# A two-layer transformer step on one core: attention's side products moved between scores and sums

## The chip, the cores and the metric

The kernel runs on one core of a Trainium2 chip, in one launch. The metric is the device time of the execution in microseconds; the median of three runs is given.

## The reference, cut to what matters

Input x has shape (2, 2048, 256). Two layers follow, each of the form x + attention(norm(x)) + ffn(norm(x)). The first has a gated linear attention and a quantised linear layer. The change lies in the second, whose attention has 16 heads of 16 columns with a linear bias by distance, one half of the heads looking back and the other forward; its other half is a mixture of 8 experts, two for each token, chosen by 20 rounds of row and column normalisation (Sinkhorn):

```
# attention
scores = einsum('bhqd,bhkd->bhqk', q, k) * (1.0 / sqrt(16)) + bias
out = einsum('bhqk,bhkd->bhqd', softmax(scores), v)
out = out.transpose(0, 2, 1, 3).reshape(B, S, D) @ Wf + bf
# experts
pi = _sinkhorn(-(xf @ gate_W.T))          # 20 rounds: rows, then columns
_, top_idx = top_k(pi, 2)
y = einsum('enf,edf->end', silu(g) * u, W_down)
out = sum over k of y[top_idx[:, k], n] * pi[:, k]
```

The second layer's result is x plus both, in float32.

## The kernel before

The span has three parts. The first layer, with the projections of the second layer's queries, keys and values at its end, takes up to about 432 us. The second layer's attention takes from there to about 830 us. The experts follow to the end.

**Units.** `_units()` (L1609) cuts the attention into 150 units. A unit has four rows, one for each head of a group of four, and each row has up to 512 query columns (`WIDE`), packed from pieces of up to 256 queries against 128 keys. The loop at L1944 to L1979 takes the units in order. Nothing reorders the work: each engine has it in the order in which the loop issues it, and for VectorE (`vector`, an `InOrder` wrapper whose calls show as L121) and most of GpSimd's sends program order is pinned. Names:

- `scores` (L1817) multiplies keys and queries for the four rows into four PSUM banks (`sc`, matmuls of L1823), and issues the exponentials on ScalarE from there to `pt` (L1832). Row 0's exponential is in two parts.
- `keep_only` (L1835) takes the minimum of the diagonal blocks of `pt` and a mask on VectorE. A unit has 0 to 12 of them.
- `weighted_sums` (L1841) multiplies `pt` by the values into one of two other banks (`o_ps`, L1846).
- `add_up` (L1860) does this for the unit two back (`LATE` is 2). Where a group of four heads has ended with that unit, it transposes the sums to `o_sb` on VectorE, and with the second group of a step it appends a chore, `normalise` (L1793), and runs its first part: reciprocal `inv`, product `on` and transposition `onT`, all on VectorE.
- `do_chore` (L1881) runs the rest of the oldest chore: the output product `f_ps` (16 recorded matmuls through `by_columns`, L1544), its addition to `acc` on VectorE and, for the second half of the heads, a store of two row tiles of the output from SP (L1815). There are 32 chores.
- `background` is the router: `DirectSinkhorn` (L1547), which in each of its 20 rounds has the steps "reciprocal of the row sums `sk_rows`, product, column sums `sk_c`" and "product with a matrix of ones into `sk_ps`, reciprocal `sk_columns`, product, next row sums `sk_r`", and then `routing.steps` (with one product, `place_ps`). `decision` follows, with one product (`d_ps`), and `sends` scatters the table's rows from GpSimd. One step is taken in a unit, and none while the masks of the unit before are more than 7 (`CALM`).
- `value_bias` (L1727) has one product, `b_ps`, a quarter of the way through.

**Banks.** PSUM has eight banks here: two for sums and six in one round, tag "mm" of the pool `ps_m` (L1713). Each new tile takes the next bank of the round, and waits until the readers of the tile that had it six tiles ago are done. Four tiles go to each unit's scores; every side product (`f_ps`, `sk_ps`, `b_ps`, `place_ps`, `d_ps`) takes one too.

**Order in a unit before.** On TensorE: scores of unit n; sums of unit n-2; the output product, if a chore was there before this unit's sums; the router's product. On VectorE: masks of unit n-1; transpositions and the chain to `onT` of unit n-2, if a group ended; the addition to `acc`; the router's or the decision's step.

Of the kernel before, what the change touches and what calls it, by code (L numbers as in the profile page):

```python
# [56 lines left out]
F32 = mybir.dt.float32  # L57
# [7 lines left out]
P = 128  # L65
B, N, E = 2, 2048, 256
# [46 lines left out]
class InOrder:  # L113


    def __init__(self, tc, engine):
        self.tc, self.engine = tc, engine
# [6 lines left out]
class LayerNorm:  # L124
# [7 lines left out]
    def tile(self, name, shape):  # L132
        name = f"ln_{name}{self.name}"
        return self.pool.tile(shape, F32, tag=name, name=name)
# [1471 lines left out]
        yield  # L1606


def _units():  # L1609

    tiles = QT // P

    def pieces_of(way, group, r, qt):  # L1620


        found = [(qt * 2 + way, 0, QT, P * way), (qt * 2 + 1 - way, P * (1 - way), P, 0)]
        slope = _slopes()[PLACES[(2 * way + group) * 4 + r] % (H1 // 2)]
        reach = math.ceil((104 + LIMIT - SHIFT) / slope) + 1
        for j in range(1, tiles * (N // QT - 1 - qt if way else qt) + 1):


            width = min(QT, reach - 1 - P * (j - 1))
            if width > 0:  # L1630
                width = -(-width // 32) * 32
                kb = qt * tiles + tiles - 1 + j if way else qt * tiles - j
                found.append((kb, QT - width if way else 0, width, None))
        return found

    steps = [(b, way, qt) for b in range(B) for way in range(2) for qt in ORDERS[way]]
    parts = [(step, group, n % 2) for n, step in enumerate(steps) for group in range(2)]
    rows = []
    for r in range(4):
        row = deque()  # L1640
        for n, ((b, way, qt), group, bank) in enumerate(parts):
            row.append((n, deque(pieces_of(way, group, r, qt))))
        rows.append(row)
    units = []
    done, begun = [[None] * len(parts) for _ in range(4)], set()
    while any(rows):
        this = len(units)
        left, masks = [deque() for _ in range(4)], []
        for r, row in enumerate(rows):
            at = slots = 0  # L1650
            while row and at < WIDE:
                n, found = row[0]
                b, way, qt = parts[n][0]
                if n >= OPEN and any(d[n - OPEN] is None or d[n - OPEN] == this for d in done):
                    break
                first = (r, n) not in begun


                def fits(width):
                    return width <= WIDE - at and max(P, width) <= SLOTS - slots  # L1660

                part = min(WIDE - at, SLOTS - slots) // P * P
                if found[0][0] == qt * 2 + way:
                    m, now = 0, found[0][2] if fits(found[0][2]) else part
                else:
                    whole = [m for m, piece in enumerate(found) if fits(piece[2])]
                    wide = whole or [m for m, piece in enumerate(found) if piece[2] - part >= P]
                    if not wide:
                        break
                    m = max(wide, key=lambda m: found[m][2])  # L1670
                    now = found[m][2] if whole else part
                if not now:
                    break
                begun.add((r, n))
                found.rotate(-m)
                kb, q0, width, diagonal = found.popleft()
                if now < width:
                    rest = None if diagonal is None else diagonal - now
                    found.appendleft((kb, q0 + now, width - now, rest))
                if not found:  # L1680
                    done[r][n] = this
                    row.popleft()
                left[r].append((r, *parts[n], kb, q0, q0 + now, at, first, not found))
                if diagonal is not None:
                    m0, m1 = max(diagonal, 0), min(diagonal + P, now)
                    if m0 < m1:
                        masks.append((r, parts[n][0][1], at + m0, m1 - m0, m0 - diagonal))
                at, slots = at + now, slots + max(P, now)
        widths = [sum(piece[6] - piece[5] for piece in pieces) for pieces in left]
        taken, pieces = [0] * 4, []  # L1690
        while any(left):
            r = min((r for r in range(4) if left[r]), key=lambda r: taken[r])
            piece = left[r].popleft()
            taken[r] += max(P, piece[6] - piece[5])
            pieces.append(piece)
        ended = [part for n, part in enumerate(parts)
                 if all(d[n] is not None for d in done) and max(d[n] for d in done) == this]
        units.append((pieces, widths, masks, ended))
    return units
# [3 lines left out]
def attention(  # L1703
# [9 lines left out]
    ps_m = ctx.enter_context(tc.tile_pool(name="aps_m", bufs=6, space=PSUM))  # L1713
    ident = c.ident

    values = operands.values
    other_values = w.tile([P, TPB, 7 * VC + HR], F32, tag="va1", name="va1")
    mask, wf, pi, grown = ready.mask, ready.wf, ready.pi, ready.grown
    for g in (2, 3):
# [7 lines left out]
    def value_bias():  # L1727


        vector.tensor_copy(ready.bvb, ready.bv.unsqueeze(2).to_broadcast([P, 2, P]))  # L1730
        yield
        ps = ps_m.tile([P, E], F32, tag="mm", name="b_ps")
        for e in range(2):
            nc.tensor.matmul(
                ps, lhsT=ready.bvb[:, e, :], rhs=wf[:, e, :], start=e == 0, stop=e == 1
            )
        vector.tensor_tensor(c.half_bias, c.half_bias, ps, ALU.add)
        vector.tensor_scalar(c.half_bias, c.half_bias, 0.5, None, ALU.mult)
        yield

    def router():
        yield from DirectSinkhorn(nc, vector, p2, ps_m, la, pi, grown, c.ones_mat).steps()
        yield from routing.steps(p2, ps_m, pi)

    def decide():
        yield from routing.blocks(p2)
# [22 lines left out]
        vector.tensor_tensor(within, within, least, ALU.mult)  # L1769
        yield  # L1770
        yield
        ps = ps_m.tile([1, P + 1], F32, tag="mm", name="d_ps")
        nc.tensor.matmul(ps[:, 0:P], lhsT=high, rhs=ident, start=True, stop=True)
        nc.tensor.matmul(
            ps[:, P : P + 1], lhsT=within, rhs=c.ones_mat[:, 0:1], start=True, stop=True
# [17 lines left out]
    def normalise(b, way, qt, turned):  # L1793


        inv = p2.tile([P, 2, QT // HR], F32, tag="inv", name="inv")
        vector.reciprocal(inv, turned[:, :, :, HD])
        on = p2.tile([P, QT // HR, 2, HD], F32, tag="on", name="on")
        vector.tensor_tensor(
            on.rearrange("p j g d -> p g j d"), turned[:, :, :, 0:HD],  # L1800
            inv.unsqueeze(3).to_broadcast([P, 2, QT // HR, HD]), ALU.mult,
        )
        onT = p2.tile([P, QT], F32, tag="onT", name="onT")
        vector.transpose(onT, on.rearrange("p j g d -> p (j g d)"))
        yield
        ts = slice(b * TPB + qt * 2, b * TPB + qt * 2 + 2)
        ps = ps_m.tile([P, 2, E], F32, tag="mm", name="f_ps")
        for n in range(2):
            by_columns(
                nc.tensor.matmul, ps[:, n, :], onT[:, n * P : (n + 1) * P], wf[:, way, :],  # L1810
                start=True, stop=True,
            )
        vector.tensor_tensor(acc[:, ts, :], acc[:, ts, :], ps, ALU.add)
        if way:
            nc.sync.dma_start(out=c.out_v[:, ts, :], in_=acc[:, ts, :])  # L1815

    def scores(pieces, widths):  # L1817
# [9 lines left out]
        for r, width in enumerate(widths):  # L1827
            ends = [at + q1 - q0 for row, *_, q0, q1, at, _, _ in pieces if row == r] if not r else []
            half = min(ends, key=lambda end: abs(end - WIDE // 2), default=width)
            for part in (slice(0, half), slice(half, width)):  # L1830
                if part.start < part.stop:
                    nc.scalar.activation(pt[:, r, part], scs[r][:, part], AF.Exp)  # L1832
        return pt

    def keep_only(pt, masks):  # L1835

# [18 lines left out]
    chores, background, sends = deque(), router(), routing.sends()  # L1855
    decision = decide()
    waiting, copies = deque(), {}
    routed, unmasked = False, None

    def add_up():  # L1860
        pieces, pt, ended = waiting.popleft()
# [19 lines left out]
    def do_chore():  # L1881
        for _ in chores.popleft():
            pass
# [58 lines left out]
    experts = Experts(tc, a, out, c, rooms, range(FULLS), range(GROUPS))  # L1942
    ahead = experts.todo[0:2]
    for n, (pieces, widths, masks, ended) in enumerate(units):  # L1944
        if n in (len(units) // 4 - 4, len(units) // 4):
            next(bias)
        if n == len(units) - BEGIN:
            for left in (background, decision, sends):
                for _ in left:
# [7 lines left out]
                block.fetch_rows()  # L1957
        if len(units) - FETCH < n <= len(units) - FETCH + 4:
            ahead[0].combine(0, range(n - len(units) + FETCH - 1, n - len(units) + FETCH))
        pt = scores(pieces, widths)  # L1960
        calm = not unmasked or len(unmasked[1]) <= CALM
        if unmasked:
            keep_only(*unmasked)
        unmasked = pt, masks
        before = len(chores)
        waiting.append((pieces, pt, ended))
        if len(waiting) > LATE:
            add_up()
        if before and chores:
            do_chore()  # L1970
        if routed:
            for _ in range(1 + n % 2):
                next(sends, None)
            if calm:
                next(decision, None)
        elif calm:
            routed = next(background, True) is True
        if n == len(units) - 4:
            ahead[0].open_rows()  # L1979
    keep_only(*unmasked)  # L1980
# [828 lines left out]
```

## Time and profile before

| | |
|---|---|
| three runs | 1500.48, 1505.16, 1506.82 us (median 1505.16) |
| profiled execution | 1507.06 us, its span 1504.8 us |
| attention's window, 432 to 830 us | PE busy 389.47, PEld 287.27, DVE 275.34, ACT 313.91 us of 398 |
| granted TensorE clock | 0.983 over the span, 0.97 in the window |
| exponentials `pt` from `sc`, 128x512 | 381 of 612 ns |
| masks on `pt`, 128x128 | 512, 283 ns each when counted singly |
| output products `f_ps` | 32 times 16 matmuls |
| Sinkhorn products `sk_ps` | 20 times 8 matmuls |
| transposition, reciprocal, product, transposition (`o_sb`, `inv`, `on`, `onT`) | 446, 254, 425, 445 ns |
| addition `acc`, 128x512 | 681 ns |

Busy time is that of the records: a matmul's end is modelled, so a busy PE is not one that never waits. PEld is TensorE's weight loads, whose starts show when the engine moved from one phase to the next. "A <- B" in a view of waits means that A was idle until B ended. Idle time of an engine that is not the bound costs nothing.

### The profile page before, as it was taken

Reading aid. Unit: us, or ns where it says so; the run is one execution under the profiler, and the core shown is the slowest. Engines: PE = TensorE matmul, PEld = TensorE weight load, DVE = VectorE, ACT = ScalarE, POOL = GpSimd, SP = SyncE. Lnnn points to the kernel's source line nnn. Section 1 sums busy time; section 2 is a strip of 40 time slices with the busy share of each in tenths; the row PEclk is TensorE's granted clock in tenths of the full one; section 3 lists DMA queues with packets and bytes.
Section 4 is the critical chain, followed back from the end, with each engine's and each line's share of the span. In section 5 each row is a group of like instructions: output and inputs, shape, how many; then the busy total and the mean of one; then the engine's idle time right before and its main releaser. Section 6 shows DMA issues by size and latency. Waiting matters only on the chain.

```text
span 1504.8 us, 33474 instructions
## 1 busy us (share of the span) xinstructions
PE 1444.7 (96%) x13712; PEld 1180.6 (78%) x13712; DVE 1009.7 (67%) x2567; ACT 730.3 (49%) x1557; POOL 538.4 (36%) x449
## 2 busy tenths in 40 slices
PE   7879999999989999999999999999999999999996
PEld 4656767676757777777666899989899998989995
DVE  6788677565448888874445767667666776666663
ACT  4444554555367888888876332333232332323231
POOL 4342222121120000399961234343434544343432
PEclk9999999999989999999999999999999999999998
DMA  8001010410353120420034656575766867576531
GB/s 236 0 15 59 30 57 30 120 58 29 81 151 60 31 62 25 95 35 5 5 131 157 224 195 199 191 286 175 261 198 218 252 210 254 193 253 241 174 83 23
DMA packets 75986, 191.94 MB, mean 128 GB/s; under 512 B 19136, under 2 KB 56768, under 8 KB 63360
## 3 DMA queue, kind: packets, MB, share of 16 engines
q0 software_dynamic: 28256, 144.23, 28.8%
q1 hardware_dynamic: 46464, 44.30, 11.9%
q8 instruction: 110, 1.80, 0.5%
q10 hardware_dynamic: 1104, 1.18, 0.3%
q14 instruction: 52, 0.43, 0.1%
HBM read 157.95 MB, written 32.10 MB: 126 GB/s over the span
## 4 chain that ended last, share of the span: by engine, by line
PE 56%; DVE 2%; ACT 1%; issue 1%; POOL 0%; POOLq 0%; another core or an unknown queue 0%
PE h_ps L121 26%; PE y_ps L121 15%; PE sc L1823 6%; PE o_ps L1846 5%; PE f_ps L1544 1%; PE h_ps L2491 1%; PE x_ps L121 1%; DVE pt L121 1%; ACT pt L1832 1%; PE h_ps L2526 0%; DVE o_sb L121 0%; ACT larger L121 0%; DVE onT L121 0%; DVE on L121 0%; DVE larger L121 0%
## 5 line engine op out<-in xcount | busy, mean ns | idle before, releaser
L1832 ACT ACTIVATE pt<-sc 128x512 f32<-128x512 f32 (+5 forms) x746 | 312.4, 517 | 78.2 <-issue 39.2
L1823 PE MATMUL sc<-qk 32*128 32x256 f32 (+3 forms) x3022 | 208.1, 361 | 3.6 <-ACT pt L1832 1.6
L121 DVE TENSOR_TENSOR larger<-larger,h_ps 128x512 f32<-128x512 f32 x160 | 109.9, 687 | 144.3 <-ACT larger L121 79.0
L1823 PEld LDWEIGHTS sc<-qk 32*128 32x128 f32 x3022 | 158.9, 189 | 46.1 <-ACT pt L1832 25.3
L121 PE MATMUL y_ps<-qk,larger 128*128 128x256 f32 x704 | 173.4, 380 | 0.3 <-DVE larger L121 0.3
L1846 PE MATMUL o_ps<-pt,va 128*32 128x256 f32 (+3 forms) x3022 | 166.2, 341 | 3.2 <-DVE o_sb L121 1.9
L121 ACT COPY larger<-h_ps 128x512 f32<-128x512 f32 x128 | 74.5, 582 | 172.7 <-PE h_ps L121 168.2
L121 DVE TENSOR_TENSOR pt<-pt,keepmask 128x128 f32<-128x128 f32 x512 | 117.4, 283 | 48.0 <-ACT pt L1832 46.9
L2405 POOL DMA_INDIRECT out<-va,to x64 | 102.7, 1604 | 124.3 <-DVE larger L121 49.1
L1846 PEld LDWEIGHTS o_ps<-pt,va 128*32 128x32 f32 x3022 | 103.3, 111 | 51.0 <-issue 20.8
L2222 POOL DMA_INDIRECT table<-rows,place x64 | 68.2, 1066 | 194.1 <-DVE pt L121 181.7
L121 PEld LDWEIGHTS y_ps<-qk,larger 128*128 128x128 f32 x704 | 123.9, 191 | 12.3 <-DVE larger L121 0.7
L121 PEld LDWEIGHTS h_ps<-va,qk 128*128 128x128 f32 x1024 | 126.6, 192 | 7.6 <-ACT larger L121 2.3
L121 PE MATMUL h_ps<-va,qk 128*128 128x128 f32 x1024 | 130.6, 276 | 1.9 <-ACT larger L121 1.9
L2568 POOL DMA_INDIRECT xb<-normed,to x64 | 65.5, 1024 | 140.5 <-DVE by L2291 71.8
L121 ACT ACTIVATE larger<-larger 128x512 f32<-128x512 f32 x64 | 40.4, 632 | 117.8 <-DVE larger L121 117.8
L121 ACT ACTIVATE va<-va 128x512 f32<-128x512 f32 x64 | 40.4, 632 | 100.2 <-DVE va L121 96.3
L121 PE MATMUL y_ps<-larger 128*128 128x256 f32 x320 | 79.0, 380 | 0.0
L121 POOL TENSOR_TENSOR pause<-ones_mat,expo 128x4 f32<-128x4 f32 x64 | 68.6, 1072 | 2.0
L121 ACT COPY va<-h_ps 128x512 f32<-128x512 f32 x64 | 36.9, 577 | 56.4 <-PE h_ps L121 51.1
L121 PE MATMUL h_ps<-larger,qk 128*128 128x128 f32 x512 | 62.7, 276 | 0.0
L121 PEld LDWEIGHTS h_ps<-larger,qk 128*128 128x128 f32 x512 | 59.7, 192 | 2.1 <-issue 2.1
(318 smaller groups left out, 2798.5 us busy)
## 6 DMA issues: line engine op xcount, KB each, us to landing
qk<-qk SPq DMA_DIRECT2D x32, 256.0 KB
qk<-qk SPq DMA_DIRECT2D x64, 128.0 KB
va<-v SPq DMA_DIRECT2D x4, 1208.0 KB
v<-v SPq DMA_DIRECT2D x8, 574.0 KB
normed<-xn SPq DMA_DIRECT2D x8, 512.0 KB
out<-acc SPq DMA_DIRECT2D x16, 256.0 KB
acc<-in_x SPq DMA_DIRECT2D x7, 512.0 KB
table<-rows,place POOLq DMA_INDIRECT x64
```

Source lines behind the costliest of these rows:

```text
L121: return lambda *a, **k: self.tc.keep_in_program_order(begin(*a, **k))
L1544: multiply(out[r : r + HR], left[:, r : r + HR], *args, **how)
L1823: nc.tensor.matmul(scs[r][:, at : at + q1 - q0], lhsT=heads[rows, 1, kb * P : (kb + 1) * P], rhs=heads[rows, 0, qt * QT + q0 : qt * QT + q ...
L1832: nc.scalar.activation(pt[:, r, part], scs[r][:, part], AF.Exp)
L1846: nc.tensor.matmul(sums[bank][r * HR : (r + 1) * HR, to + q0 : to + q1], lhsT=values[b, way][:, kb, h * VC : h * VC + HR], rhs=pt[:, r, at ...
L2222: send = self.tc.keep_in_program_order(self.nc.gpsimd.indirect_dma_start(out=self.c.table, in_=self.rows[:, t, :], in_offset=None, out_off ...
L2405: send = e.nc.gpsimd.indirect_dma_start(out=e.out, in_=y[:, c, :], in_offset=None, out_offset=bass.IndirectOffsetOnAxis(ap=self.to[:, c : ...
L2491: self.e.nc.tensor.matmul(ps[rows, :], lhsT=self.xT[:, c * P + r * SB : c * P + (r + 1) * SB], rhs=self.w[:, r, at : at + ST], start=c == ...
L2568: self.nc.gpsimd.indirect_dma_start(out=to, out_offset=None, in_=self.c.normed, in_offset=bass.IndirectOffsetOnAxis(ap=at, axis=0),)
```

## The change

A small class, `Spare`, stands in for the pool where side products ask for a bank. While a unit is worked on it holds the banks of rows 2 and 3 of the scores of the unit before; a side product takes the first that is left, and where there is none it takes one of the round as before. The list is emptied at the end of each unit. The six banks of the round thus go to scores alone, and in the order of the round the spare banks are those that the next unit's rows 0 and 1 take.

The order in a unit changes too. The bias product, the router's or the decision's step and then the chore come right after the masks, all ahead of `add_up`. So on TensorE it is now: scores of unit n, router's product, output product, sums of unit n-2. On VectorE: masks of unit n-1; router's or decision's step; addition to `acc`; transpositions and chain of unit n-2.

```diff
+class Spare:
+    def __init__(self, pool):
+        self.pool, self.banks = pool, []
+
+    def tile(self, shape, dt=F32, tag=None, name=None):
+        if not self.banks:
+            return self.pool.tile(shape, dt, tag=tag, name=name)
+        bank = self.banks.pop(0)[0 : shape[0], 0 : math.prod(shape[1:])]
+        return bank if len(shape) == 2 else bank.rearrange("p (a b) -> p a b", a=shape[1])
...
-    values = operands.values
+    values, spare = operands.values, Spare(ps_m)
...
-        ps = ps_m.tile([P, E], F32, tag="mm", name="b_ps")
+        ps = spare.tile([P, E], F32, tag="mm", name="b_ps")
...
-        yield from DirectSinkhorn(nc, vector, p2, ps_m, la, pi, grown, c.ones_mat).steps()
-        yield from routing.steps(p2, ps_m, pi)
+        yield from DirectSinkhorn(nc, vector, p2, spare, la, pi, grown, c.ones_mat).steps()
+        yield from routing.steps(p2, spare, pi)
...
-        ps = ps_m.tile([1, P + 1], F32, tag="mm", name="d_ps")
+        ps = spare.tile([1, P + 1], F32, tag="mm", name="d_ps")
...
-        ps = ps_m.tile([P, 2, E], F32, tag="mm", name="f_ps")
+        ps = spare.tile([P, 2, E], F32, tag="mm", name="f_ps")
...
-        return pt
+        return pt, scs
...
     for n, (pieces, widths, masks, ended) in enumerate(units):
-        if n in (len(units) // 4 - 4, len(units) // 4):
-            next(bias)
...
-        pt = scores(pieces, widths)
+        pt, scs = scores(pieces, widths)
+        spare.banks, behind = [bank for bank in behind[2:] if bank is not None], scs
         calm = not unmasked or len(unmasked[1]) <= CALM
         if unmasked:
             keep_only(*unmasked)
         unmasked = pt, masks
-        before = len(chores)
-        waiting.append((pieces, pt, ended))
-        if len(waiting) > LATE:
-            add_up()
-        if before and chores:
-            do_chore()
+        if n in (len(units) // 4 - 4, len(units) // 4):
+            next(bias)
         if routed:
             for _ in range(1 + n % 2):
                 next(sends, None)
             if calm:
                 next(decision, None)
         elif calm:
             routed = next(background, True) is True
+        if chores:
+            do_chore()
+        waiting.append((pieces, pt, ended))
+        if len(waiting) > LATE:
+            add_up()
+        spare.banks = []
```

More of the change, by code (lines that the diff above doesn't have):

```diff
@@ L1857, in attention @@
     waiting, copies = deque(), {}
-    routed, unmasked = False, None
+    routed, unmasked, behind = False, None, []
     def add_up():
```

## The prediction

> **What bounds the kernel now.** I read the page first, then the windows of the attention stage (432 to 830 us, all that the change touches), then who waited for whom there, then the timeline around single side products.
>
> ```profile
> span 1504.8 us, 33474 instructions
> PE 1444.7 (96%) x13712; PEld 1180.6 (78%) x13712; DVE 1009.7 (67%) x2567; ACT 730.3 (49%) x1557; POOL 538.4 (36%) x449
> ```
>
> PE is the bound over the whole span, and 56% of the chain that ended last is PE. After attention PE goes straight into the experts, so a microsecond lost by PE in attention is lost at the end. Two stretches of attention, at full clock, one with the 20 Sinkhorn products and one without:
>
> ```profile
> core 0: us, PE busy (x) PEld busy (x) DVE busy (x) ACT busy (x) POOL busy (x), PEclk, DMA share, GB/s
> 447.97:553.49 105.52, 103.67 (x1878) 75.72 (x1875) 87.72 (x281) 84.24 (x201) 0.00 (x0) 1.00 0.30 53
> 636.08:767.53 131.45, 130.88 (x2334) 96.72 (x2330) 71.75 (x267) 111.74 (x267) 118.49 (x113) 1.00 0.14 22
> ```
>
> The reader is to see that PE's busy time hides its stalls (its ends are modelled), so I count from start to start of the weight loads (PEld). Undisturbed, scores take 1.08 us and sums 1.00 us. The first stretch holds 40 units: seven with an output product f_ps (25.67 us) and 33 others (79.85 us, 2.42 each). The second holds 54 units: ten with an f_ps (32.02 us, 3.20 each) and 44 others (99.43 us, 2.26 each). A plain unit is 0.18 us above PE's own 2.08, because scores wait for ScalarE to finish exponentials and free banks:
>
> ```profile
> PEld sc L1823 <- ACT pt L1832: 25.3, 73, 1.4
> PEld o_ps L1846 <- issue: 20.8, 63, 0.9
> ...
> PEld sk_ps L1544 <- ACT pt L1832: 4.0, 6, 0.7
> PEld o_ps L1846 <- DVE pt L121: 2.7, 7, 0.7
> ...
> PEld f_ps L1544 <- ACT pt L1832: 2.7, 6, 0.8
> ```
>
> What a side product in the round costs, from the timeline (start, us, engine):
>
> ```profile
> 494.69 0.19 PEld L1544 LDWEIGHTS sk_ps<-sk_c,ones_mat 128*32 128x32 f32 x8 [0.19 <-issue]
> 494.90 1.61 PE L1823 MATMUL sc<-qk 32*128 32x256 f32 x20
> 495.38 0.73 PEld L1823 LDWEIGHTS sc<-qk 32*128 32x128 f32 x14 [0.17 <-ACT pt L1832]
> 496.20 2.02 ACT L1832 ACTIVATE pt<-sc 128x256 f32<-128x256 f32 x5 [0.38 <-ACT pt L1832]
> ```
>
> The scores after the Sinkhorn product stall in their middle, since they need one bank more of the unit just scored, and ScalarE then stands idle. And what an output product needs:
>
> ```profile
> 757.40 1.00 PEld L1823 LDWEIGHTS sc<-qk 32*128 32x128 f32 x18
> 757.57 0.45 DVE L121 STREAM_TRANSPOSE o_sb<-o_ps 128x256 f32<-128x256 f32 x1 [0.66 <-PE o_ps L1846]
> 758.05 0.25 DVE L121 RECIPROCAL inv<-o_sb 128x16 f32<-128x16 f32 x1
> 758.34 0.42 DVE L121 TENSOR_TENSOR on<-o_sb,inv 128x256 f32<-128x256 f32 x1
> 758.72 0.59 PEld L1846 LDWEIGHTS o_ps<-pt,va 128*32 128x32 f32 x20 [0.32 <-issue]
> 758.80 0.45 DVE L121 STREAM_TRANSPOSE onT<-on 128x256 f32<-128x256 f32 x1
> 759.40 0.77 PEld L1544 LDWEIGHTS f_ps<-cwf,onT 128*32 128x32 f32 x16
> 760.59 0.96 PEld L1823 LDWEIGHTS sc<-qk 32*128 32x128 f32 x24 [0.41 <-ACT pt L1832]
> 760.73 0.69 DVE L121 TENSOR_TENSOR acc<-acc,f_ps 128x512 f32<-128x512 f32 x1 [1.49 <-PE f_ps L1544]
> ```
>
> Here the last sums hand over at 757.40, VectorE's chain of four ends at 758.80+0.45 = 759.25, scores end at 758.72. Today the sums of the next unit (758.72 to 759.40) cover that difference.
>
> **The change part by part.** It adds and removes no instruction; it moves them.
>
> *Sinkhorn products leave the round.* 101 scores after plain sums take 1.25 us (median), 19 after a Sinkhorn product 1.53, 23 after an output product 1.09. Upper end of the gain: all that the first stretch has over the second, 33 x (2.42-2.26) = 5.3 us, plus its f units, 25.67 - 1.06 (a bias product that stays) - 7 x 3.20 = 2.2 us; together 7.5 us. Lower end: those 7.5 less the products' own 20 x 0.21 = 4.2 us if PE still pays them, 3.3 us. A product's 0.21 us fits mostly into the 0.18 us that PE waits for ScalarE anyway, but its operand sk_c must now be there one sum (1.00 us) earlier: masks (0.2 to 0.28 us each, up to 7) and reciprocal, product, reduction (0.33+0.43+0.62 us) end about 2.1 us after the exponentials of the unit before last, about when scores end. I take a gain of 5 us.
>
> *Output products leave the round.* After them scores take 1.09 us, no stall: the 1 us of f_ps already gave ScalarE its time. Gain 0.
>
> *Output products stand before the sums.* Program order puts the chain to onT at the end of one unit and f_ps right behind the next unit's scores. For the first 30 of the 32 (the last two are not in the loop's steady order) I set the end of onT against the end of scores in the trace: onT ends 1.81 us (median) after the handover of the sums it comes from, scores end after 1.20 us. The differences, none below zero counted, sum to 18.3 us; 29 are positive. Where f_ps waits today it starts 0.11 us behind onT: 29 x 0.11 = 3.2 us. So 21.5 us, of which today's 1.3 us of waits for onT are no new loss: +20. PE waits in order, the sums and next scores stand behind it, ScalarE has no new scores and is idle, so nothing hides it: in the f unit today ScalarE is already through before the next scores come.
>
> *Router steps move ahead of the chain on VectorE.* The Sinkhorn and routing steps were issued after add_up and now come before it. In seven of the first eight f steps a half iteration (sk_rows, pi, sk_c 1.38 us, or sk_columns, pi, sk_r 1.04 us) now precedes the chain. VectorE stood idle 0 to 0.42 us before the chain there, which absorbs part: the pushes are 1.38, 1.04, 1.12, 0.96, 1.16, 1.06, 1.29, 8.0 us. In the next eleven f steps nine have a routing or deciding step before the chain (0.4 to 1.2 us each, the 1024-wide comparison 1.22), some 5 us net of idle time. Together up to 13; zero if the chain is early for other reasons. The product ahead of f_ps (0.2 us) hides some. I take 8.
>
> *The bank comes back earlier in the order.* The spare bank is the one that the next scores take first (row 0). They start one sum (1.00 us) after f_ps ends; the addition into acc needs about 0.15 + 0.69 us after f_ps, so 0.15 us are left. Where masks keep VectorE (today acc starts 1.33 us after f_ps by the median, 1.5 to 2.9 us in ten steps), scores wait. Summed over those ten, above 1.33: 5 us; but the later f_ps gives VectorE time. I take 2, ends 0 and 12 (0.4 us at each of 30).
>
> *Other queues.* On SP a store of out and a qk load change places; loads wait long there anyway, off PE's path: 0. POOL's sends and ScalarE's order are unchanged: 0. Bias and decision products (1.06 us and 0.34 us, once each): below 0.5 either way.
>
> **Two rules against the rows.** By the row, the 25.3 us for which score loads wait on ScalarE are mostly the plain round's own balance. The Trainium skill, "Perfetto Trace Analysis", Optimization Strategy, says that the same gap repeating on the engine that should be saturated can mean too little PSUM for the next tile; that would credit the change with 25.3+4.0+2.7 = 32 us and end 2 us faster even against my 30 of losses. The stretch without Sinkhorn products still shows 2.26 a unit, so I keep 5. Speaking against the change: the granted clock is 1.00 in both stretches above. "TensorE: Matmul & The Clock Gate", Why this matters for your kernels, warns that PE gaps beyond some 3 us halve the clock. The longest wait I derive is 1.37+1.38 = 2.8 us; by the rows it adds 0, by the rule a half-clock window of 3.4 us (an estimate from that page) loses 1.7 us. I take 0.
>
> **Sum.** -5 + 20 + 8 + 2 = +25 us. Profiled: span 1504.8, time 1507.06, so 2.26 around it; 1504.8 + 25 + 2.26 = 1532.1. That run is 1.9 us above the median of the runs, 1505.16, so I predict 1530.
>
> **The rivals.** *Waits for onT take the banks' place* (mine): 0.70, from 1518 (gain 7.5, waits 20, no pushes: +13) to 1540 (gain 3.3, waits 20, pushes 13, bank 5: +35).
>
> *The spare bank comes back late as well*: each f step costs 0.4 us more at the next scores, +12 on top of +28 to +30: 1545. For it: 0.15 us of slack. Against: f_ps itself is later, VectorE then free. 0.11.
>
> *A wash*: what PE loses before f_ps is mostly made up by shorter scores later. If each 0.18 us stall of the two plain units after an f step went, 30 x 0.36 = 11 us would come back, and with no pushes +2 to +6 is left: 1509. Against: today's f unit is followed by 1.09, then about 1.39 us scores; the stall comes back at once. 0.10.
>
> *Faster*: the bank round is the only loss that counts. The 7.5 us come in full, and VectorE, no longer waiting for f_ps behind the sums, starts the chain early enough. It decides where onT ends within 1.1 us of the handover; then f_ps loses nothing and 1497.7 results. Against: the chain alone is 0.45+0.25+0.42+0.45 = 1.57 us, longer than 1.2 us of scores. 0.09.
>
> **How the numbers follow.** What a measurement of this kernel tells from no change is about 0.5%, 7.5 us. The main case and the late bank are slower by more; of the wash about 0.01 is beyond, of the faster case 0.01 within. Slower 0.82, same 0.10, faster 0.08. Range 1512 to 1544: it leaves out the faster case, half of the wash and some of the late bank.
>
> **What would show it.** PE's weight loads of f_ps wait for onT, some 0.7 us in most of 30 steps, 1.5 and more in the first ten; today it is 1.3 us in three. Scores after a Sinkhorn product fall from 1.53 to 1.2 us; plain units stay near 2.25 us; f units go from 3.2 to about 4. The experts' part keeps its length. Wrong if the waits for onT total below 12 us, or if attention ends before 830 us.

## The result, and the profile after

The changed kernel takes 1522.39 us (median of 4 runs, 1517.14 to 1523.14), the kernel before, in runs beside it, 1502.82 us (4 runs, 1499.79 to 1506.82). The ratio, estimated over the single runs and not from the two medians, is 1.0121, 95% interval 1.0085 to 1.0158: slower by more than the 0.5% that can be told. The profiled execution took 1522.3 us. Its page:

```profile
span 1520.5 us, 33472 instructions
PE 1444.8 (95%) x13712; PEld 1179.8 (78%) x13712; DVE 1012.4 (67%) x2567; ACT 730.2 (48%) x1557; POOL 541.8 (36%) x449
```

The reader is to see the same PE busy time as before (1444.8 us against 1444.7) in a span that is 15.7 us longer: no work was added, PE waits more. The windows of the same units as those shown before (in the second, the same place in the order of units, but 53 units for 54):

```profile
core 0: us, PE busy (x) PEld busy (x) DVE busy (x) ACT busy (x) POOL busy (x), PEclk, DMA share, GB/s
448.26:557.00 108.74, 104.08 (x1878) 73.39 (x1875) 89.55 (x283) 83.86 (x200) 0.00 (x0) 1.00 0.28 52
645.89:781.13 135.24, 129.25 (x2290) 95.74 (x2286) 70.45 (x260) 109.21 (x262) 121.82 (x115) 1.00 0.12 18
```

In the first window, with equal weight loads (1875), PE is busy for 0.4 us more and the stretch takes 3.22 us more; the clock is 1.00 in both. The second is one unit shorter than before (2286 loads against 2330), so all comparisons below are made over the same units, from the start of a unit's first weight load to that of a later unit's. The product of `value_bias`, 1.06 us once, lies in an f unit of the first row before and in another unit after; it is in the totals, and taken out of the means of both kernels:

| stretch | before | after |
|---|---|---|
| 40 units with the Sinkhorn products | 105.51: 7 f units of 3.51, 33 others of 2.42 | 108.73: 7 f units of 4.20, 33 others of 2.37 |
| the 86 units behind them | 211.72: 18 f units of 3.24, 68 others of 2.255 | 224.14: 18 f units of 3.98, 68 others of 2.243 |
| the next 16 units | 50.82 | 48.79 |

An "f unit" is one with an output product. The f units carry the loss, 7 x 0.69 and 18 x 0.74, together 18 us. The others give some back, 33 x 0.05 and 68 x 0.012, together 2.4 us. The last row holds long stalls on weight fetches that wander from run to run, and I read nothing from it. The loads' waits in attention, 430 to 850 us (the product's tile is now called `sc`, since it lies in a bank of the scores; L1544, the line of output and Sinkhorn products both, tells them from the scores, L1836):

```profile
PEld sc L1836 <- ACT pt L1845: 22.6, 68, 1.0
PEld sc L1544 <- ACT pt L1845: 20.0, 21, 1.8
PEld sc L1836 <- issue: 19.5, 76, 1.3
...
PEld sc L1544 <- issue: 4.4, 11, 0.8
PEld sc L1544 <- DVE onT L121: 4.3, 8, 1.3
```

and those of the matmuls themselves:

```profile
PE sc L1544 <- DVE onT L121: 14.1, 19, 1.6
```

Scores still wait for ScalarE for 22.6 us (25.3 before), and the products have got a wait of their own. The view of the loads gives 20.0 us of it to ScalarE's `pt`, the view of the matmuls gives it to `onT`. The timeline decides (start, us, engine; the number in brackets is the idle time before):

```profile
772.50 1.00 PEld L1836 LDWEIGHTS sc<-qk 32*128 32x128 f32 x18
773.10 0.45 DVE L121 STREAM_TRANSPOSE o_sb<-o_ps 128x256 f32<-128x256 f32 x1 [0.82 <-PE o_ps L1859]
773.59 0.25 DVE L121 RECIPROCAL inv<-o_sb 128x16 f32<-128x16 f32 x1
773.87 0.42 DVE L121 TENSOR_TENSOR on<-o_sb,inv 128x256 f32<-128x256 f32 x1
774.33 0.45 DVE L121 STREAM_TRANSPOSE onT<-on 128x256 f32<-128x256 f32 x1
774.89 0.62 PEld L1544 LDWEIGHTS sc<-cwf,onT 128*32 128x32 f32 x16 [1.40 <-ACT pt L1845]
775.57 0.80 PEld L1859 LDWEIGHTS o_ps<-pt,va 128*32 128x32 f32 x20
776.12 0.69 DVE L121 TENSOR_TENSOR acc<-acc,sc 128x512 f32<-128x512 f32 x1 [1.34 <-PE sc L1544]
776.78 0.96 PEld L1836 LDWEIGHTS sc<-qk 32*128 32x128 f32 x24 [0.41 <-issue]
```

The sums hand over at 772.50 and scores have their last load by 773.50. The chain to `onT` ends at 774.33+0.45 = 774.78, and the product starts 0.11 us later, at 774.89. In 29 of the first 30 output products the first load comes no more than 0.12 us behind the end of `onT`: it is `onT` that they wait for. The sums, which used to fill that time, come behind it at 775.57. The next scores start at 776.78, when the addition to `acc` (776.12 to 776.81) is just ending, and do not stall on it.

And a Sinkhorn product now:

```profile
509.60 0.31 PEld L1836 LDWEIGHTS sc<-qk 32*128 32x128 f32 x6 [0.20 <-issue]
509.81 0.61 DVE L121 TENSOR_REDUCE sk_c<-pi 128x8 f32<-128x256 f32 x1
510.30 0.75 PEld L1836 LDWEIGHTS sc<-qk 32*128 32x128 f32 x16 [0.40 <-ACT pt L1845]
511.36 0.16 PEld L1544 LDWEIGHTS sc<-sk_c,ones_mat 128*32 128x32 f32 x8 [0.31 <-DVE pt L121]
511.41 0.81 PEld L1859 LDWEIGHTS o_ps<-pt,va 128*32 128x32 f32 x20
512.43 1.02 PEld L1836 LDWEIGHTS sc<-qk 32*128 32x128 f32 x22 [0.20 <-ACT pt L1845]
```

The stall in the middle of the scores is still there (0.40 us at 510.30), now in the scores ahead of the product, not in those behind it. `sk_c` ends at 510.42, almost a microsecond before the product.

### The profile page after: what moved, and what is told of

Its sections match the earlier page's. It is cut to its first block, busy times and chain, and to the rows that moved or that the text cites. A ratio compares the mean times of both kernels' runs of the same rounds, so it can differ in the third digit from the quotient of the medians.

```text
span 1520.5 us, 33472 instructions
## 1 busy us (share of the span) xinstructions
PE 1444.8 (95%) x13712; PEld 1179.8 (78%) x13712; DVE 1012.4 (67%) x2567; ACT 730.2 (48%) x1557; POOL 541.8 (36%) x449
## 3 DMA queue, kind: packets, MB, share of 16 engines
q10 hardware_dynamic: 1104, 1.18, 0.3%
## 4 chain that ended last, share of the span: by engine, by line
PE 48%; DVE 1%; ACT 1%; issue 0%; POOL 0%; POOLq 0%
PE h_ps L121 26%; PE y_ps L121 14%; PE sc L1836 2%; PE o_ps L1859 2%; PE h_ps L2505 1%; PE x_ps L121 1%; PE sc L1544 1%; PE h_ps L2540 0%; ACT pt L1845 0%; DVE o_sb L121 0%; DVE on L121 0%; ACT va L121 0%; ACT larger L121 0%; DVE onT L121 0%; PE h_ps L2528 0%
## 5 line engine op out<-in xcount | busy, mean ns | idle before, releaser
L1836 PE MATMUL sc<-qk 32*128 32x256 f32 (+4 forms) x3022 | 209.4, 359 | 3.8 <-ACT pt L1845 1.7
L1836 PEld LDWEIGHTS sc<-qk 32*128 32x128 f32 x3022 | 158.9, 188 | 49.5 <-ACT pt L1845 22.6
L1859 PEld LDWEIGHTS o_ps<-pt,va 128*32 128x32 f32 x3022 | 107.1, 110 | 42.4 <-issue 14.5
L2582 POOL DMA_INDIRECT xb<-normed,to x64 | 69.3, 1084 | 152.9 <-DVE wt L2310 75.8
```

Of the source, the lines that this page charges most:

```text
L1836: nc.tensor.matmul(scs[r][:, at : at + q1 - q0], lhsT=heads[rows, 1, kb * P : (kb + 1) * P], rhs=heads[rows, 0, qt * QT + q0 : qt * QT + q ...
L1859: nc.tensor.matmul(sums[bank][r * HR : (r + 1) * HR, to + q0 : to + q1], lhsT=values[b, way][:, kb, h * VC : h * VC + HR], rhs=pt[:, r, at ...
L2582: self.nc.gpsimd.indirect_dma_start(out=to, out_offset=None, in_=self.c.normed, in_offset=bass.IndirectOffsetOnAxis(ap=at, axis=0),)
```

## The experiments

My theory after the result: the wait of the output products for `onT` is the whole loss, since they lost the sums that covered the chain. Rivals: the lent bank comes back late; the router's steps push VectorE's chain. And one question beside: where did the 5 us credited to the Sinkhorn products go?

**e1_ripe: everything as after, but a chore is done only if it was there a unit earlier.** The product is still between scores and sums and in a lent bank; the chain has a whole unit to end.

```diff
 ...
-        if chores:
+        if ripe:
             do_chore()
+        ripe = len(chores)
```

> The changed kernel, but a chore waits one unit longer, so that onT is made two units before its output product and TensorE never has to wait for it. Theory (the wait for onT behind one unit's scores is the loss: 0.7 us in each of some 29 units): the output products' units fall from about 3.9 to 3.2 us, 19 us come back, 1503 us, 1498 to 1508. Rival (the spare bank, which the next scores take first, comes back late, or the router's steps ahead of the chain cost): the time stays at 1516 to 1525.

Measured: 1506.42 us (12 runs) beside 1505.66 of before, ratio 1.0008 (0.9993 to 1.0022); no difference. The f units of the 86 take 3.32 us instead of 3.98. Its timeline around an output product:

```profile
757.32 1.00 PEld L1836 LDWEIGHTS sc<-qk 32*128 32x128 f32 x18
758.64 0.59 PEld L1859 LDWEIGHTS o_ps<-pt,va 128*32 128x32 f32 x20 [0.32 <-issue]
758.72 0.45 DVE L121 STREAM_TRANSPOSE onT<-on 128x256 f32<-128x256 f32 x1
759.64 0.30 PEld L1836 LDWEIGHTS sc<-qk 32*128 32x128 f32 x6 [0.41 <-ACT pt L1845]
760.13 0.79 PEld L1836 LDWEIGHTS sc<-qk 32*128 32x128 f32 x18 [0.19 <-ACT pt L1845]
761.04 0.59 PEld L1544 LDWEIGHTS sc<-cwf,onT 128*32 128x32 f32 x16
```

`onT` is ready at 759.17, 1.87 us ahead of its product. The view of the loads' waits has no line with `onT` any more:

```profile
PEld sc L1836 <- ACT pt L1845: 27.2, 90, 1.1
...
PEld sc L1544 <- ACT pt L1845: 3.2, 10, 0.5
```

So the loss goes with this one wait, with the place of the products unchanged and their banks lent as before.

**e2_output_only: as after, but the bias, router and decision stand behind `add_up` again,** and take a bank of the round. Only the output product is moved.

```diff
+        if chores:
+            do_chore()
+        waiting.append((pieces, pt, ended))
+        if len(waiting) > LATE:
+            add_up()
+        spare.banks = []
         if n in (len(units) // 4 - 4, len(units) // 4):
             next(bias)
 ...
-        if chores:
-            do_chore()
-        waiting.append((pieces, pt, ended))
-        if len(waiting) > LATE:
-            add_up()
-        spare.banks = []
```

> Only the output and bias order of the change: the chore stands between scores and sums in a spare bank, the router's and the decision's steps are after the sums, in the round, as before. Theory: the waits for onT are all there, 29 times 0.7 us, and the Sinkhorn stretch costs what it did before: 1503 + 20 = 1523, 1518 to 1528. Rival (the router's steps that now stand ahead of VectorE's chain are a third of the loss): 1511 to 1516.

Measured: 1522.93 us (4 runs), ratio 1.0101 (1.0074 to 1.0129): all of the loss. The 40 units take 106.99 us (108.73 after, 105.51 before, all with the bias product), the 86 take 223.52 (224.14 after). The wait is the same one:

```profile
PE sc L1544 <- DVE onT L121: 12.5, 19, 1.4
```

The router's move is worth 1.7 us net in the stretch where it acts, and cannot be seen in the total.

**e3_router_only: the reverse.** Router, bias and decision stand between scores and sums, in lent banks; the output product is behind the next unit's sums and in the round, as before.

```diff
-        ps = spare.tile([P, 2, E], F32, tag="mm", name="f_ps")
+        ps = ps_m.tile([P, 2, E], F32, tag="mm", name="f_ps")
 ...
-        if chores:
-            do_chore()
+        before = len(chores)
         waiting.append((pieces, pt, ended))
         if len(waiting) > LATE:
             add_up()
+        if before and chores:
+            do_chore()
```

> Only the router's part of the change: its products between scores and sums in spare banks, the output products after the sums in the round as before. Theory: what the scores after a Sinkhorn product no longer wait for ScalarE, the product itself now waits for sk_c, so no gain: 1503, 1500 to 1505. Rival of the prediction (sk_c is there in time): 5 us faster, 1495 to 1499. Rival (its steps make the chain to onT late even where the product stands after the sums): 1507 to 1512.

Measured: 1503.16 us (20 runs) beside 1505.66, ratio 0.9984 (0.9973 to 0.9994). It is the one version that is faster than both kernels, and by only 2.5 us. In its trace the 40 units take 104.03 us, 1.5 less than before, and the 86 behind them 214.03, 2.3 more, so the two stretches do not place the gain. The theory was that the product waits for `sk_c`, and it fails: 18 of the 20 products start 0.26 us or more behind the end of `sk_c`. One of them:

```profile
491.64 0.56 PEld L1836 LDWEIGHTS sc<-qk 32*128 32x128 f32 x6 [0.21 <-ACT pt L1845]
492.38 0.62 DVE L121 TENSOR_REDUCE sk_c<-pi 128x8 f32<-128x256 f32 x1
492.46 0.72 PEld L1836 LDWEIGHTS sc<-qk 32*128 32x128 f32 x10 [0.26 <-ACT pt L1845]
493.52 0.16 PEld L1544 LDWEIGHTS sc<-sk_c,ones_mat 128*32 128x32 f32 x8 [0.33 <-issue]
```

`sk_c` ends at 493.00, half a microsecond early. The scores ahead of the product are long (491.64 to 493.18), and they wait for exponentials.

**e4_round_banks: the order of after, without the lent banks.** One line goes; every side product takes a bank of the round.

```diff
-        spare.banks, behind = [bank for bank in behind[2:] if bank is not None], scs
```

> The order of the changed kernel, but every side product takes a bank of the round. Theory: the order makes the loss, the banks only a small gain on 20 Sinkhorn products (0.2 to 0.4 us each): 1522 + 5 = 1527, 1522 to 1532. Rival (the spare bank makes the loss, since the next scores take it first): 1503 to 1512.

Measured: 1521.89 us (4 runs), ratio 1.01 (1.0079 to 1.0122), the same as after. The f units of the 86 take 3.94 us (3.98 after). Waits of matmuls and of loads:

```profile
PE f_ps L1544 <- DVE onT L121: 17.1, 22, 1.6
```
```profile
PEld f_ps L1544 <- ACT pt L1845: 25.8, 25, 1.8
```

With no bank lent there is none to come back late: that rival falls for this kernel. The order alone makes the loss; the banks, which the change is about, make no difference to the total time. In the 40 units they do: these take 107.10 us without the lent banks and 108.73 with them. More on this below.

**e5_no_products: what do the 20 Sinkhorn products cost?** The kernel before, without `sk_ps`; the reciprocal reads the column sums of each partition instead of their sum over all partitions.

```diff
-            total = self.psum.tile([P, NE], F32, tag="mm", name="sk_ps")
-            by_columns(nc.tensor.matmul, total, self.ones_mat, csum, start=True, stop=True)
-            vector.reciprocal(of_columns[:, n, :], total)
+            vector.reciprocal(of_columns[:, n, :], csum)
```

> The kernel before without the 20 Sinkhorn products: the column sums are not added over the partitions, so the reciprocals are taken of sk_c (the output is another). Nothing of theirs is left on TensorE or in the banks. If the prediction's credit was right (the stretch with these products is slower than the one without because of their bank and their time), plain units there fall from 2.42 to about 2.26 us and the time by 5 to 7.5 us, to 1496 to 1499. If the stretch is slower for another reason (its own scores waiting for ScalarE), the units stay at 2.37 or more and the time falls by 0 to 2.5 us, to 1501 to 1504.

With these column sums left unfinished the tokens fall on the experts differently, and the experts then take their general way; the total of 6.3 ms is no answer, and only units of attention are read. The 40 take 97.30 us instead of 105.51 (f units 3.23 for 3.51 without the bias product, the others 2.230 for 2.420). So the products did cost 8.2 us, near the 7.5 that the prediction set as the upper end of the gain, and the change recovers little of it. How far single traces can be compared is seen here too: the 86 units, which this edit leaves alone, take 215.19 us in this trace and 211.72 before, and two neighbouring units hold all of the difference.

**Where it went.** The built programs show which bank each tile has. Both the prediction and the description ahead of it took the six banks to be handed out in a fixed turn. They are not: a tile gets the bank whose readers are done first in the order as built. ScalarE's order is the builder's too, not the loop's: a unit's exponentials stand there by rows 0, 2, 3, 1 in one unit and 1, 2, 0, 3 in another. A lent bank has one reader more, so it is done late and is passed over. Times of scores in the 40 units, by how many exponentials of the unit before they need (units next to an output product left out, and in after and e3_router_only one unit that needs four):

| | two needed | three needed |
|---|---|---|
| before | 19, median 1.09 us | 14, median 1.67 us |
| after | 15, median 1.24 us | 10, median 1.71 us |
| e3_router_only | 20, median 1.26 us | 12, median 1.71 us |
| e4_round_banks | 22, median 1.29 us | 4, median 1.54 us |

Before, all 14 units that need a third exponential follow a Sinkhorn product: it took a bank, so they take three of the unit just scored instead of two. After, three of the 10 are of that kind; the other seven have the product behind their own scores. The bank that will be lent to it would have been free with the first or second exponential, and the scores take that of the third in its place.

So the lending is what keeps the number up: with the same order and no lent bank (e4_round_banks) it falls from 14 to 4. The 33 other units, without the bias product, take 2.42 us before, 2.30 in e4_round_banks and 2.37 after. In these units the order gains 3.9 us, and lending the banks gives 2.3 of them back. A kernel with the order of e3_router_only and all banks from the round was not run. The passing over would also explain why the late bank never showed: a bank that is not taken is not waited for.

**e6_halves: a smaller output product.** As e1_ripe, but each half of `f_ps` in a unit of its own, with its own addition, to fit into the slack of a plain unit.

```diff
-        ps = spare.tile([P, 2, E], F32, tag="mm", name="f_ps")
         for n in range(2):
+            ps = spare.tile([P, E], F32, tag="mm", name="f_ps")
 ...
-        vector.tensor_tensor(acc[:, ts, :], acc[:, ts, :], ps, ALU.add)
+            row = acc[:, ts.start + n, :]
+            vector.tensor_tensor(row, row, ps, ALU.add)
+            if not n:
+                yield
 ...
```

> The kernel whose chore waits one unit longer, with each output product in two halves of 0.5 us, one a unit, each with its own addition (0.4 us instead of one of 0.69). Theory: a plain unit has 0.2 us in which TensorE waits for ScalarE, so each half costs 0.3 us instead of the whole product's 0.95: 29 x 0.35 = 10 us faster than that kernel, 1493 to 1498, faster than both. Rival (the second addition and the second change between products eat it, or scores wait as often as before): 1502 to 1508.

A miss: 1514.14 us (6 runs), ratio 1.0068 (1.0046 to 1.0091). A unit with a half takes 2.95 us and the plain ones 2.305, so each half costs 0.65 us, where 0.3 us was expected. TensorE's own part of that is 0.43 us (0.24 of loads, and sums behind it of 1.19 us instead of 1.00). The rest, some 0.2 us, is in the scores ahead, as with a whole product (1.39 us in the median here, 1.40 in e1_ripe, where plain scores take 1.21): it comes once for each product, whatever its size, and there are now twice as many. Scores still wait:

```profile
PEld sc L1839 <- ACT pt L1848: 28.1, 90, 0.9
...
PEld sc L1839 <- DVE acc L121: 3.8, 6, 1.6
```

That it is the lending that costs these 0.2 us agrees with the table above, where e4_round_banks isolates it for Sinkhorn products; for output products it was not isolated.

**Three kernels with a strict turn.** If the passing over eats the gain, six banks in a strict turn should bring it back. `Round` asks for them by number; ScalarE's exponentials are pinned to program order.

```diff
+class Round:
+    def __init__(self, pool):
+        self.pool, self.n = pool, 0
+
+    def tile(self, shape, dt=F32, tag=None, name=None):
+        self.n += 1
+        return self.pool.tile(shape, dt, tag=f"mm{self.n % 6}", name=name, bufs=1)
 ...
-    ps_m = ctx.enter_context(tc.tile_pool(name="aps_m", bufs=6, space=PSUM))
+    ps_m = Round(ctx.enter_context(tc.tile_pool(name="aps_m", bufs=1, space=PSUM)))
 ...
-                    nc.scalar.activation(pt[:, r, part], scs[r][:, part], AF.Exp)
+                    scalar.activation(pt[:, r, part], scs[r][:, part], AF.Exp)
 ...
+    scalar = InOrder(tc, nc.scalar)
```

e7_round_kept is e3_router_only with it:

> The kernel with the router's part alone (e3), with the six banks given out strictly in turn and the exponentials in row order. In the changed kernel and in e3 the pool gives a lent bank back last, so that the scores of a neighbouring unit take three banks of the unit just scored and wait for its third exponential; such scores took 1.7 us against 1.25 us, 11 or 12 of them in the Sinkhorn stretch. In strict turn no unit there needs the third but the one after an output product. Theory (the lent bank is still taken out of the round): those 11 fall to 1.25 us, some 5 us less than e3, 1496 to 1500. Rival (the product's own place between scores and sums costs it, whichever bank): 1502 to 1505.

A miss: 1512.82 us (6 runs) beside 1505.29, ratio 1.0055 (1.0037 to 1.0074). The scores ahead of a Sinkhorn product do fall, to 1.34 us in the mean of 20 (1.49 in e3_router_only), but other waits come:

```profile
PEld sc L1847 <- ACT pt L121: 28.4, 81, 1.9
...
PEld o_ps L1870 <- DVE o_sb L121: 4.9, 6, 1.8
...
PEld f_ps L1544 <- DVE sk_columns L121: 3.3, 6, 1.1
```

The output product meets a bank that was lent to a Sinkhorn product, and plain units grow from 2.255 to some 2.3 us. e8_round_before, the kernel before with the same edit, tells how much of this is the edit's own:

> The kernel before with the banks strictly in turn and the exponentials in row order, nothing else: the control of e7. Scores after a Sinkhorn product need the third exponential as they did. Theory: no change, 1502 to 1507. Rival (the turn itself or the order of exponentials is what helps): 1496 to 1500.

Measured: 1509.55 us (10 runs), ratio 1.0023 (1.0006 to 1.0040), plain units 2.304 us; 1502 to 1507 us was expected. The edit by itself, the strict turn and the pinned exponentials together, costs about 4 us, and 0.05 us in a plain unit of this trace. e9_ripe_round is e1_ripe with it:

> The kernel whose chore waits one unit longer (e1), with the banks strictly in turn: the changed kernel without both of its faults, neither waits for onT nor a bank taken out of the round. Theory: e1's 1506 less 5 us in the Sinkhorn stretch, 1499 to 1503, and units after an output product as fast as before. Rival (a bank that comes back to row 0 or 1 of the next scores too late for the addition to acc): 1506 to 1512.

Measured: 1507.57 us (10 runs), ratio 1.0024 (1.0010 to 1.0038): a miss of the theory, and where the rival, the late bank, had put it. Its loads wait:

```profile
PEld sc L1847 <- ACT pt L121: 17.3, 61, 0.9
PEld sc L1847 <- DVE acc L121: 14.3, 26, 1.9
```

Waits for ScalarE fall by 10 us against e1_ripe (27.2), and in the 40 units no scores need a third exponential. In their place scores wait 26 times for the addition to `acc`, which still reads the lent bank: 14.3 us. Here the prediction's late bank is seen, and its size is near the 12 us given to it. In the changed kernel the pool avoids it by skipping the bank, and pays with the third exponential.

## Why the prediction was right

**The waits for `onT`: right in mechanism, place and size; less of them reaches the total.** I had +20 for 29 products, from setting the end of the chain against the end of scores in the trace of before. 25 of them lie in the two stretches read, a share of 25/29 x 20 = 17.2 us. With the router left behind the sums (e2_output_only) the idle time of the loads just ahead of these 25 products goes from 7.5 to 24.4 us, 16.8 more; after, it is 23.7. The units grow by less: in e2_output_only the 18 f units of the 86 by 0.68 us each, as forecast, and the seven of the 40 by only 0.26 (bias product left out), together 14.0 us. "Nothing hides it" fails in these seven. The idle time ahead of their output products does grow, by 4.2 us, but six of them hold a Sinkhorn product too, and the idle time ahead of that falls from 3.5 to 0.2 us: the sums now stand between the two products and cover the wait of the second. That the wait for `onT` is the loss is shown by e1_ripe: with the product a unit later, the loss is gone. The f units of the 86 went from 3.24 to 3.98 us against "from 3.2 to about 4".

**The router's push: mis-sized.** I took 8 us, with 1 us and more in each of the first f steps. What after has over e2_output_only in its f units is 7 x 0.42 + 18 x 0.06 = 4 us, of which other units of the 40 give some back (net 1.7 us there), and nothing shows in the total. In the seven, `onT` does come later, by 4.3 us in all, but the wait ahead of the output product does not grow with it (5.6 us idle after, 6.4 in e2_output_only): the waits in scores and ahead of the Sinkhorn product, which now both stand before it, have grown instead (4.1 us for 1.1). So these 4 us are not the push that I had reckoned.

**The bank that comes back late: nothing here.** I had 2, ends 0 and 12. e4_round_banks has none to come back and takes the same time. The mechanism exists (e9_ripe_round, 14.3 us), where the banks have a fixed turn. The 1545 that this rival was given also leaves out the gain of 5; with it the sum is +35, or 1540.

**The Sinkhorn products: wrong in the step, and the gain too large.** I had -5, between 3.3 and 7.5. Their cost is 8.2 us (e5_no_products); of it the change keeps 1.6 us in the 33 other units. The forecast that scores after a product fall from 1.53 us to 1.2 came true (now 1.1 to 1.3), but the scores ahead of it rose from about 1.15 to 1.6 us, and to only 1.3 in e4_round_banks. The failed step is "leave the round": the lent bank drops out of the round all the same, now for the scores ahead of the product. What gains in these units is the order, and it gains more with no bank lent. The rival that the change does not do what it says belonged in the list.

**The sum** was +25 us, and the span grew by 15.7; the medians of the runs lie 19.6 us apart side by side, and 16.7 us against the 31 later runs of before (1505.66). Waits and pushes, 28 in the sum, are 18 in the f units; the late bank, 2, is nothing; of the gain of 5, 2.4 us came in the other units. 18 - 2.4 is 15.6, the growth of the two stretches; what lies outside them cancels. The forecast of 1530 lies 7.6 us above the 1522.39 measured, within the range. Each of the three losses came out smaller in the total, and so did the gain: that the errors offset one another in part is luck.

**The wash and the faster case** fall: scores after the f units give nothing back (68 other units at 2.243 us for 2.255), and in none of the first 30 output steps does `onT` come within 1.1 us of the handover: the earliest needs 1.18 us, the median 1.84.

**The two rules.** "Too little PSUM" ("Perfetto Trace Analysis", Optimization Strategy, as the prediction told it) would have credited 32 us. Neither the lent banks (e4_round_banks against after) nor e3_router_only, at 1.5 us in its stretch, came near it: the repeating gap of 25.3 us is in the main not the products' banks. Whether more banks than these eight would close it, no run here shows. For the clock, the waits of up to 1.8 us in the view left it at 1.00 in both windows, and at 0.986 over the span (0.983 before): the 0 was right. No wait of TensorE in these windows came near the 3 us of the rule, so the rule itself stands untested here.

## What to carry to other kernels

A product that is put ahead of other work on its engine loses that work as cover: set the end of its operands' chain against the new slot, step by step, before counting what the move frees. If the slot is worth having, let the consumer run one unit later, as e1_ripe does, at no cost in instructions. A buffer that is lent out counts as busy in the pool that owns it, also for tiles asked for ahead of the borrower; look at which buffer each tile is given in the built program before crediting a buffer with being free. And try the order without the buffers, as e4_round_banks does: here the two parts of one change worked against each other.

## What the hardware showed that I had not expected

The loads of a product do not show all that it takes from TensorE: sums behind an output product take 1.19 to 1.22 us from their first load to the next scores, against 1.00, for a whole product (0.67 us of loads) and for a half (0.24 us) alike, so a half costs 0.43 us and a whole 0.87. And giving the six banks out in a fixed turn, with the exponentials in program order, costs 0.05 us in a plain unit (e8_round_before, 2.304 us for 2.255 in one trace each); which of the two does it was not separated.
